# A conv, attention and expert kernel: the per-image matrix in twelve steps, another order of the set-up, and moved places in the slot

## The chip, the cores and the metric

The kernel runs on one core of a Trainium2 chip, from one launch. The metric is the time on the device in microseconds (us), lower is better. Each stated time of a kernel is the median of several runs.

## What is computed

The input x is 8 images of 56 x 56 pixels with 256 channels in float32, so 25,088 tokens of 256 numbers. Two layers follow each other. In the reference, cut to what matters:

```python
def _path(x, w1, ..., v3):                      # 32 of them, 4 inner channels each
    h = relu(_bn(einsum('nhwc,cd->nhwd', x, w1) + b1, ...))
    h = relu(_bn(conv3x3(h, w2) + b2, ...))
    return relu(_bn(einsum('nhwd,dc->nhwc', h, w3) + b3, ...))
x = relu(paths.sum(axis=0) + x)                 # layer 0

k, v = _layernorm(qkv, ...), _layernorm(qkv, ...)   # per head of 32 channels, q = qkv
kv = einsum('bhnd,bhne->bhde', k, v) / N            # one 32 x 32 matrix per head and image
out = einsum('bhnd,bhde->bhne', q, kv) + x          # attention without a softmax

probs = softmax(tokens @ router_w.T)                # 8 experts, the best 2 per token
for e in range(E):
    out = out + combine[:, e:e+1] * (gelu(tokens @ w1[e] + b1[e]) @ w2[e] + b2[e])

t = t + attention(_ln_t(t))                         # layer 1
t = t + experts(_ln_t(t))
```

## The kernel before, in words

**Tiles and slots.** The tokens are cut into 56 chunks of 448 (8 rows of an image, 7 chunks per image). The program is a loop over slots s (L1494 on). Slot s holds, interleaved: the third convolution (conv3) of chunk s as 32 `pair` steps (L631, products L643, relu on ACT L648, second relu and sum on DVE L651) with their sums on PE (`sum_paths`, L664, result u at L671); the first convolution (conv1, L265) of chunk s+2: transposes tx of the loaded xi (L276) and product c1 (L287); the taps R (L301) and the 3 x 3 convolution (conv2, L323) of chunk s+1, whose result is split in two parts and sent by DMA into hl (`halves`, L334); the end of chunk s-1 (`end_steps`, L693): transposes tu (L712), statistics per head, a power on POOL (L777), the inverse (up to L799), the scale on POOL (L803), and the products kv (L813), summed per image into kvs; and the attention of chunk a = s-8 (`attn_steps`, L920). Slots 0 to 7 have no attention; their places are those with "alone" in the name. Slots from 56 on have no convolution any more; they are the tail.

**Experts.** After attention, chunks are routed in groups of up to two (`route_steps`, L1018): DVE computes ranks up to rboth (L1067), PE multiplies it (rk, L1074), and rows go out to the experts' regions by indirect DMA from POOL (L1120). When a group of chunks is closed a plan (`plan_steps`, L1135, its run lists L1235 to L1256) makes the table of tiles of 128 rows. `moe_steps` then passes tiles through the experts' weights (te L1335, ph L1375, py L1391 and L1395), and the rows go back by indirect DMA (L1413).

**An image's matrix.** At slots 8, 15, 22, ..., 57 chunk a is the first of its image, and `image_steps` (L831) turns kvs into one 256 x 256 matrix in two halves f of 128 channels. `keys` (L835) makes, for each half, a diagonal matrix Arow of the channel sums (L847), its product with ones on PE (sv, L848), and with eight operations on DVE (L852 to L864) the half's A. Arow and At have one buffer each. `matrix` (L867) multiplies A by the mean and transposes it (cs, L872, and AT), and fills the table tab. `router` (L887) multiplies AT by the router's weights (ar), copies, multiplies by the mean (arm), subtracts. tab is what attention reads at L939.

**What sets the order.** PE, ACT and DVE run in the order in which the program issues (`manual_schedule`); POOL, SP and the DMA queues are ordered by the scheduler. Each list of steps gets places, fractions of the slot, from the dictionary `places` (L598 on): `at` gives each step its own place, other lists are spread by cost between two places, and `issue` sorts all steps of the slot by place and calls them. `after` in `places` says how many tile passes are left for each slot of the tail (`tiles_by`). PSUM has a pool of 7 buffers for all products but the sums.

**Set-up.** Before slot 0 the weights are loaded and laid out (W2s at L233 in twelve DMAs on the queue of SP), chunks 0 and 1 pass conv1, the mask and scale of the third weights are made (tp_mask, tp_g at L383, W3s at L384, tp_w at L391), then the table of the third bias (b4 at L414, tp_b3 at L419), and then conv2 of chunk 0. After that come the other tables, among them the centred router weights (tp_rw, L480). `load` (L84) fetches a chunk of x into xi.

Of the kernel before, what the change touches and what calls it, by code (L numbers as in the profile page):

```python
# [8 lines left out]
F32 = mybir.dt.float32  # L9
# [16 lines left out]
def kernel(  # L26
# [32 lines left out]
    P = 128  # L59
# [20 lines left out]


    xs_in = {}

    def load(s):  # L84
        b, c = divmod(s, NCH)
        X = xin.tile([T, KT, C], F32, tag="xi", name=f"xi_{s}")
        nc.sync.dma_start(
            out=X, in_=x[b, c * CH : (c + 1) * CH, :].rearrange("(k q) c -> q k c", q=T)
        )
        xs_in[s] = X  # L90

    xtp = ctx.enter_context(tc.tile_pool(name="xtp", bufs=4))
# [137 lines left out]
    W2s = setup.tile([3 * 32, NG, 3, D], F32, name="W2s")  # L230
    for dx in range(3):
        for g in range(NG):
            nc.sync.dma_start(  # L233
                out=W2s[dx : 3 * 32 : 3, g],
                in_=W2[32 * g : 32 * g + 32].rearrange(
                    "q (dy dx o) -> dx q dy o", dy=3, dx=3
                )[dx],
            )
# [76 lines left out]
    def conv2_steps(s):  # L315
# [19 lines left out]
        def halves():  # L335

            h2 = h2s[s]
            hi = split.tile([P, CH], F32R, tag="hi", name=f"hi_{s}")
            lo = split.tile([P, CH], F32R, tag="lo", name=f"lo_{s}")
            nc.vector.tensor_copy(hi, h2)  # L340
            nc.vector.tensor_tensor(lo, h2, hi.bitcast(F32), ALU.subtract)
# [46 lines left out]
    for ab in range(NQ):  # L388
# [9 lines left out]
            ALU.mult,  # L398
        )


    pmod = setup.tile([NP, NPL], F32, name="pmod")
    nc.vector.tensor_reduce(
# [12 lines left out]
        )  # L416
    tp = ps_mm.tile([P, 512], F32, tag="mm", name="tp_b3")
    for cg in range(NCG):
        nc.tensor.matmul(  # L419
            tp[:, cg * 8 : cg * 8 + 8],  # L420
            b4[:, cg].rearrange("q p c -> q (p c)"), pdiv, start=True, stop=True,
        )
    nc.vector.tensor_copy(b3t, tp[:, : NCG * 8].rearrange("q (g n) -> q g n", n=8))
    nc.vector.tensor_scalar_mul(nb3, b3t, -1.0)
    all_of(conv2_steps(0))

    for f in range(NF):
        tp = ps_mm.tile([P, 512], F32, tag="mm", name=f"tp_sb_{f}")
# [26 lines left out]
    tables = ctx.enter_context(tc.tile_pool(name="tables", bufs=1))  # L455


    def column(src, name):

        t = const.tile([P, NF], F32, name=name)  # L460
        nc.sync.dma_start(out=t, in_=src.rearrange("o (f c) -> c (o f)", c=P))
        return t

    def bcast(src, name):
        t = const.tile([P, C], F32, name=name)
        nc.sync.dma_start(out=t, in_=src.to_broadcast([P, C]))
        return t

    kw_c, kb_c = column(kw, "kw_c"), column(kb, "kb_c")
# [4 lines left out]
    nc.gpsimd.memset(mean_of, 1.0 / C)  # L474

    rwc = const.tile([P, NF, E], F32, name="rwc")
    nc.sync.dma_start(out=rwc, in_=rwT.rearrange("(f c) e -> c f e", c=P))
    tp = ps_mm.tile([P, 512], F32, tag="mm", name="tp_rw")
    for f in range(NF):
        nc.tensor.matmul(tp[:, :E], mean_of, rwc[:, f, :], start=(f == 0), stop=(f == NF - 1))  # L480
    for f in range(NF):
        nc.vector.tensor_sub(rwc[:, f, :], rwc[:, f, :], tp[:, :E])

# [106 lines left out]
    def unordered(ins, group, keep=()):  # L590
# [7 lines left out]


    places = {  # L600
        "after": [7, 5, 5, 5, 6, 5, 5, 5, 10],
        "attention": [0.108, 0.243, 0.378, 0.514, 0.622, 0.689, 0.744, 0.798, 0.881, 0.881],
        "attention first": [0.396, 0.487, 0.578, 0.669, 0.742, 0.953, 0.953, 0.953, 0.953, 0.989],
        "attention last": [
            0.151, 0.272, 0.393, 0.514, 0.611, 0.611, 0.657,
            0.706, 0.754, 0.791, 0.815, 0.839, 0.863, 0.912,
        ],
        "attention first last": [
            0.611, 0.692, 0.774, 0.856, 0.921, 0.962, 0.982,
            0.982, 0.982, 0.982, 0.982, 0.982, 0.982, 0.982,  # L610
        ],
        "conv1": [0, 0, 0.111],
        "conv1 alone": [0, 0.011, 0.024],
        "conv2": [0.615, 0.615, 0.655, 0.675],
        "conv2 alone": [0.607, 0.613, 0.613, 0.761],
        "end": [0.109, 0.151, 0.211, 0.242, 0.337, 0.431, 0.551, 0.681, 0.761, 0.908],
        "end alone": [0.143, 0.178, 0.188, 0.248, 0.328, 0.408, 0.408, 0.658, 0.752, 0.887],
        "fetch": [0.119],
        "image": [0.001, 0.107, 0.214],
        "tiles": [0.043, 0.2, 0.99],  # L620
        "conv3": [0.7, 0.9],
        "plan": [0.569, 0.983],
        "route": [0, 0.368],
        "route last": [0, 0.254],
        "scatter": [0.302, 0.551],
        "scatter last": [0.35],
        "taps": [0.144],
        "taps alone": [0.391],
    }

    unit, sums = {}, {}  # L631
# [199 lines left out]
    def image_steps(b):  # L831

        v = {}

        def keys():  # L835
            kv = kvs.pop(b)

            G3 = v["A"] = one.tile([P, NF, P], F32, tag="A", name=f"A_{b}")
            rows = one.tile([P, P], F32, tag="Arow", name=f"Arow_{b}")
            ps = ps_mm.tile([P, NF, P], F32, tag="mm", name=f"sv_{b}")  # L840
            for f in range(NF):

                g = kv[:, f, f : f + P]
                s = kv[:, f, P : P + 1] if f == 0 else kv[:, f, 0:1]
                vw, vb = vw_b[:, f * P : (f + 1) * P], vb_b[:, f * P : (f + 1) * P]

                nc.vector.tensor_scalar_mul(rows, ident, s)  # L847
                nc.tensor.matmul(ps[:, f, :], ones_f, rows, start=True, stop=True)  # L848

                A = G3[:, f, :]  # L850
                t = one.tile([P, P], F32, tag="At", name=f"At_{b}_{f}")
                nc.vector.tensor_mul(A, g, vw)  # L852
                nc.vector.scalar_tensor_tensor(A, vb, s, A, op0=ALU.mult, op1=ALU.add)
                nc.vector.tensor_scalar_mul(A, A, kw_c[:, f : f + 1])
                nc.vector.tensor_mul(t, vw, ps[:, f, :])
                nc.vector.scalar_tensor_tensor(t, vb, float(N), t, op0=ALU.mult, op1=ALU.add)
                nc.vector.scalar_tensor_tensor(
                    A, t, kb_c[:, f : f + 1], A, op0=ALU.mult, op1=ALU.add
                )
                nc.vector.scalar_tensor_tensor(  # L860
                    A, A, 1.0 / N, head_mask.rearrange("q h c -> q (h c)"),
                    op0=ALU.mult, op1=ALU.mult,
                )
                nc.vector.tensor_add(A, A, ident)  # L864

        def matrix():
            A = v["A"]  # L867
            ps = ps_mm.tile([P, NF, P], F32, tag="mm", name=f"cs_{b}")
            pt = ps_mm.tile([P, NF, P], F32, tag="mm", name=f"AT_{b}")
            AT = v["AT"] = one.tile([P, NF, P], F32, tag="AT", name=f"ATs_{b}")  # L870
            for f in range(NF):
                nc.tensor.matmul(ps[:, f, :], mean_of, A[:, f, :], start=True, stop=True)  # L872
                nc.tensor.transpose(pt[:, f, :], A[:, f, :], ident)
            tab = v["tab"] = one.tile(
                [P, NF, C + 2 * E], F32, tag="tab", name=f"tab_{b}", bufs=2
            )
            nc.vector.tensor_copy(AT, pt)
            for f in range(NF):
                for g in range(NF):
                    dst = tab[:, f, g * P : (g + 1) * P]  # L880
# [4 lines left out]
                nc.vector.tensor_copy(tab[:, f, C + E :], rwc[:, f, :])  # L885

        def router():  # L887
            AT, tab = v["AT"], v["tab"]
            ps = ps_mm.tile([P, 512], F32, tag="mm", name=f"ar_{b}")
            AR = one.tile([P, NF, E], F32, tag="AR", name=f"AR_{b}")  # L890
            for f in range(NF):
                nc.tensor.matmul(
                    ps[:, f * E : (f + 1) * E], AT[:, f, :], rwc[:, f, :], start=True, stop=True
                )
            nc.vector.tensor_copy(AR, ps[:, : NF * E].rearrange("q (f e) -> q f e", e=E))
            pm = ps_mm.tile([P, 512], F32, tag="mm", name=f"arm_{b}")
            for f in range(NF):
                nc.tensor.matmul(
                    pm[:, :E], mean_of, AR[:, f, :], start=(f == 0), stop=(f == NF - 1)
                )  # L900
            for f in range(NF):
                nc.vector.tensor_sub(tab[:, f, C : C + E], AR[:, f, :], pm[:, :E])
            tables_of[b] = tab

        return [(1.0, keys), (1.5, matrix), (1.0, router)]


    fetched, Xs, pays, logits = {}, {}, {}, {}
# [587 lines left out]
    for s in range(S + A + 1):  # L1496
# [116 lines left out]
```

## Time and profile before

| what | value |
|---|---|
| median of 3 runs | 3165.85 us (3164.92 to 3170.51) |
| the profiled run | 3194.13 us |
| its span in the trace | 3192.3 us, 1.83 us less than the run |
| granted PE clock, mean over the span | 0.962 |
| busy: PE, DVE, ACT, POOL | 92%, 68%, 60%, 58% of the span |
| set-up, 0 to 53 us | PE busy 27.39 us, PE clock 0.70 |
| tail, 2560 to 3192 us | PE busy 538.94 of 632 us |

In the profile PE is the matrix engine and PEld its loading of weights, DVE the vector engine, ACT the scalar engine, POOL the GpSimd engine and SP the engine that issues most DMAs. A row such as "L651 DVE ... x1792 | 1131.2, 677 | 446.4 <-ACT r L648 414.4" gives the line of the code, the engine, the operation, the count, the busy us and the mean ns of one; then the idle us of the engine just before such operations and what ended most of it. A row of the timeline gives start, length, and in brackets the idle time before it and what ended that. The profiled run is 0.9% above the median, so durations are read within its own span.

### The profile page before, as it was taken

What the parts mean: (1) busy time and instruction counts of PE and PEld (TensorE: products, weight loads), DVE (VectorE), ACT (ScalarE), POOL (GpSimd) and SP (SyncE); (2) the same over time, 40 slices, a digit from 0 to 9 for tenths busy, and PEclk for the clock granted to TensorE, in tenths of its full rate; (3) what the DMA queues carried; (4) which work ended last, traced back from release to release, by engine and by line L of the source; (5) the groups of instructions that cost most, each with busy time, mean ns of one, the idle gap of its engine ahead of it and who ended that gap; (6) DMA issues with size and microseconds to landing.
All of it is one profiled execution on the core that took longest, in us unless ns stands there. A gap on an engine that the chain in (4) does not pass through costs nothing.

```text
span 3192.3 us, 53679 instructions
## 1 busy us (share of the span) xinstructions
PE 2924.8 (92%) x16677; PEld 1663.9 (52%) x16677; DVE 2173.6 (68%) x5743; ACT 1919.8 (60%) x3827; POOL 1844.5 (58%) x1363
## 2 busy tenths in 40 slices
PE   6999888888999999999999999999999997887798
PEld 3334334333455555455555555555555555776677
DVE  4787887787877687776877777777778784433200
ACT  2666665556666666566666766566656654454455
POOL 1233254455566675756756666666663556677677
PEclk7999998899999999999999999999999998998899
DMA  2543344344556666667665766667756666898897
GB/s 68 156 127 123 120 133 127 112 146 152 158 163 163 190 175 177 168 177 192 184 184 155 203 184 169 179 164 197 191 161 181 176 160 152 210 250 205 202 223 179
DMA packets 322669, 537.53 MB, mean 168 GB/s; under 512 B 41152, under 2 KB 232784, under 8 KB 322384
## 3 DMA queue, kind: packets, MB, share of 16 engines
q1 hardware_dynamic: 239808, 429.91, 44.4%
q0 software_dynamic: 81984, 103.45, 17.8%
q8 instruction: 133, 2.18, 0.3%
q14 instruction: 152, 1.25, 0.1%
q10 hardware_dynamic: 592, 0.76, 0.1%
HBM read 248.01 MB, written 192.55 MB: 138 GB/s over the span
## 4 chain that ended last, share of the span: by engine, by line
PE 68%; DVE 10%; issue 4%; ACT 3%; POOL 3%; DMA 2%; another core or an unknown queue 0%; ACTq 0%; SPq 0%; POOLq 0%; DVEq 0%
PE c L643 12%; PE ph L1375 11%; PE su L664 11%; PE py L1395 9%; PE at L939 7%; PE kv L813 3%; DVE r L651 3%; PE te L1335 3%; PE c L323 2%; PE py L1391 2%; POOL hsd L777 2%; PE c L287 2%; ACT r L648 2%; PE tu L712 1%; PE tx L276 1%
## 5 line engine op out<-in xcount | busy, mean ns | idle before, releaser
L651 DVE SCALAR_TENSOR_TENSOR r<-c,nb,r 128x448 f32<-128x448 f32 x1792 | 1131.2, 677 | 446.4 <-ACT r L648 414.4
L648 ACT ACTIVATE r<-c,b3t 128x448 f32<-128x448 f32 x1792 | 1038.5, 634 | 333.0 <-PE c L643 314.9
L1413 POOL DMA_INDIRECT out_dram<-y,index x420 | 660.5, 1573 | 342.7 <-ACT y L1399 221.5
L643 PE MATMUL c<-hl,W3hl 64*128 64x448 f32 x3584 | 690.4, 427 | 52.7 <-ACT r L648 19.3
L1120 POOL DMA_INDIRECT regions<-pay,rrowi x448 | 428.9, 957 | 311.9 <-PE c L643 198.5
L664 PE MATMUL su<-r,gather 128*32 128x448 f32 x3584 | 558.0, 566 | 42.8 <-DVE r L651 34.6
L643 PEld LDWEIGHTS c<-hl,W3hl 64*128 64x128 f32 x3584 | 328.2, 188 | 482.6 <-issue 242.0
L1375 PE MATMUL ph<-eT,w 128*128 128x256 f32 x1680 | 453.2, 401 | 38.1 <-issue 15.1
L1399 ACT ACTIVATE y<-py,rows 128x256 f32<-128x256 f32 x420 | 196.7, 474 | 438.9 <-PE py L1395 327.8
L1395 PE MATMUL py<-w,hT 128*128 128x256 f32 x1680 | 432.0, 381 | 7.0 <-issue 6.3
L1375 PEld LDWEIGHTS ph<-eT,w 128*128 128x128 f32 x1680 | 306.0, 196 | 169.0 <-issue 77.0
L1379 ACT ACTIVATE hT<-ph,w 128x256 f32<-128x256 f32 x420 | 197.9, 476 | 252.2 <-PE ph L1375 127.6
L777 POOL TENSOR_TENSOR hsd<-hsd,half 112x36 f32<-112x36 f32 x49 | 303.3, 6190 | 70.5 <-DVE hsd L775 69.6
L1395 PEld LDWEIGHTS py<-w,hT 128*128 128x128 f32 x1680 | 290.3, 191 | 36.6 <-issue 7.5
L939 PE MATMUL at<-tab,tT 128*112 128x272 f32 x896 | 266.2, 421 | 15.1 <-ACT r L648 6.1
L738 POOL TENSOR_TENSOR norm<-t,hmean 112x512 f32<-112x512 f32 x112 | 121.4, 1164 | 245.5 <-PE c L643 125.0
L664 PEld LDWEIGHTS su<-r,gather 128*32 128x32 f32 x3584 | 101.6, 109 | 250.2 <-DVE r L651 107.9
L939 PEld LDWEIGHTS at<-tab,tT 128*112 128x112 f32 x896 | 150.8, 182 | 94.1 <-issue 33.1
L943 DVE SCALAR_TENSOR_TENSOR X<-at,rs,X 112x256 f32<-112x256 f32 x224 | 107.0, 478 | 122.4 <-PE at L939 60.8
L1391 PE MATMUL py<-b2hl,own 128*128 128x256 f32 x420 | 179.1, 426 | 6.7 <-ACT y L1399 2.8
L1065 POOL TENSOR_TENSOR rq<-ebase,rq 112x8 f32<-112x8 f32 (+1 forms) x32 | 51.2, 1600 | 227.0 <-DVE rq L1064 227.0
L1339 ACT COPY eT<-te 128x512 f32<-128x512 f32 x210 | 123.5, 588 | 60.5 <-PE te L1335 40.6
(261 smaller groups left out, 3160.4 us busy)
## 6 DMA issues: line engine op xcount, KB each, us to landing
w<-Wd SPq DMA_DIRECT2D x210, 513.0 KB
rows<-regions SPq DMA_DIRECT2D x210, 259.0 KB
xi<-in_x_dram SPq DMA_DIRECT2D x56, 448.0 KB
hl<-hi SPq DMA_DIRECT2D x112, 224.0 KB
tTs<-u SPq DMA_DIRECT2D x56, 448.0 KB
ts<-t SPq DMA_DIRECT2D x56, 448.0 KB
tT<-tTs SPq DMA_DIRECT2D x56, 448.0 KB
X<-ts SPq DMA_DIRECT2D x56, 448.0 KB
```

Of the source, the lines that this page charges most:

```text
L643: product = nc.tensor.matmul(tiles[g][:, :CH], W3hl[rows, ab, cg, :], hl[rows, ab, :], start=True, stop=True)
L648: nc.scalar.activation(r, tiles[0][:, :CH], AF.Relu, bias=b3t[:, cg, 2 * ab : 2 * ab + 1])
L651: nc.vector.scalar_tensor_tensor(r, tiles[1][:, :CH], nb3[:, cg, 2 * ab + 1 : 2 * ab + 2], r, op0=ALU.max, op1=ALU.add,)
L664: nc.tensor.matmul(ps[32 * c4 : 32 * c4 + 32, :CH], gather, unit.pop((s, 4 * u + c4)), start=(ab == 0), stop=(ab == NQ - 1),)
L777: nc.gpsimd.tensor_tensor(sd, sd, half[:T, :].rearrange("q (k h) -> q k h", k=KT), ALU.pow)
L939: nc.tensor.matmul(ps, tT[:, f, k * T : (k + 1) * T], tables_of[b][:, f, :], start=(f == 0), stop=(f == NF - 1),)
L1120: ins = nc.gpsimd.indirect_dma_start(out=regions[n], out_offset=bass.IndirectOffsetOnAxis(ap=v["row_i"][:, (m - group[0]) * KT + k, n : n ...
L1375: nc.tensor.matmul(ps, w[:, f * C + hf * P : f * C + (hf + 1) * P], eT[:, f, :], start=(f == 0), stop=(f == NF - 1),)
L1379: nc.scalar.activation(hT[:, hf, :], ps, AF.Gelu, bias=w[:, 2 * NF * C + hf : 2 * NF * C + hf + 1])
L1391: nc.tensor.matmul(ps, own.to_broadcast([P, P]), b2hl, start=True, stop=False)
L1395: nc.tensor.matmul(ps, hT[:, f, h * P : (h + 1) * P], w[:, (NF + f) * C : (NF + f + 1) * C], start=False, stop=(f == NF - 1),)
L1413: ins = nc.gpsimd.indirect_dma_start(out=out_rows, out_offset=at, in_=y[:, h, :], in_offset=None, compute_op=ALU.add, **partial,).ins
```

## The change

It has three parts.

1. `image_steps` returns twelve steps in place of three, each with a place of its own from 0.001 to 0.294 of the slot (before: 0.001, 0.107, 0.214). The diagonal matrices of both halves are made in the first step, in two buffers (the tags Arow and At), and both products sv follow in the second. No operation is added or left out.
2. Set-up: the twelve W2s DMAs are issued from POOL instead of SP. `conv2_steps(0)` is called before the table of the third bias. The load of chunk 3 waits for the split of chunk 0's conv2 (`halved`). The loads of kw, kb, vw, vb and of the router's weights wait for the last product of the bias table (`not_yet`). The centring of the router's weights moves to the start of slot 1.
3. Places: conv1 and conv2 with and without attention, the ends, attention, taps, plan, route, scatter and tiles, and the tile passes left for the tail (`after`, the sum goes from 53 to 52).

```diff
+        ins = nc.sync.dma_start(
             out=X, in_=x[b, c * CH : (c + 1) * CH, :].rearrange("(k q) c -> q k c", q=T)
-        )
+        ).ins
+        if s == 3:
+            tc.add_manual_dep(ins, halved[0].name, SYNC, reason="not needed by the first chunk")
...
-            nc.sync.dma_start(
+            nc.gpsimd.dma_start(
...
+            if s == 0:
+                halved.append(ins)
...
+    all_of(conv2_steps(0))
...
+    last_made = product.ins
     nc.vector.tensor_copy(b3t, tp[:, : NCG * 8].rearrange("q (g n) -> q g n", n=8))
     nc.vector.tensor_scalar_mul(nb3, b3t, -1.0)
-    all_of(conv2_steps(0))
...
+    def not_yet(ins):
+        tc.add_manual_dep(ins, last_made.name, SYNC, reason="not needed by the first chunk")
...
+    def center_router():
+        tp = ps_mm.tile([P, 512], F32, tag="mm", name="tp_rw")
+        for f in range(NF):
+            nc.tensor.matmul(tp[:, :E], mean_of, rwc[:, f, :], start=(f == 0), stop=(f == NF - 1))
+        for f in range(NF):
+            nc.vector.tensor_sub(rwc[:, f, :], rwc[:, f, :], tp[:, :E])
...
-        "after": [7, 5, 5, 5, 6, 5, 5, 5, 10],
-        "attention": [0.108, 0.243, 0.378, 0.514, 0.622, 0.689, 0.744, 0.798, 0.881, 0.881],
-        "attention first": [0.396, 0.487, 0.578, 0.669, 0.742, 0.953, 0.953, 0.953, 0.953, 0.989],
+        "after": [7, 5, 5, 3, 6, 5, 6, 5, 10],
+        "attention": [0.108, 0.235, 0.378, 0.514, 0.579, 0.689, 0.744, 0.798, 0.881, 0.94],
+        "attention first": [0.396, 0.487, 0.578, 0.669, 0.742, 0.953, 0.99, 0.99, 0.99, 0.99],
         "attention last": [
-            0.151, 0.272, 0.393, 0.514, 0.611, 0.611, 0.657,
-            0.706, 0.754, 0.791, 0.815, 0.839, 0.863, 0.912,
+            0.19, 0.311, 0.432, 0.553, 0.65, 0.65, 0.65,
+            0.693, 0.741, 0.778, 0.802, 0.938, 0.938, 0.938,
         ],
         "attention first last": [
             0.611, 0.692, 0.774, 0.856, 0.921, 0.962, 0.982,
             0.982, 0.982, 0.982, 0.982, 0.982, 0.982, 0.982,
         ],
         "conv1": [0, 0, 0.111],
-        "conv1 alone": [0, 0.011, 0.024],
-        "conv2": [0.615, 0.615, 0.655, 0.675],
-        "conv2 alone": [0.607, 0.613, 0.613, 0.761],
-        "end": [0.109, 0.151, 0.211, 0.242, 0.337, 0.431, 0.551, 0.681, 0.761, 0.908],
-        "end alone": [0.143, 0.178, 0.188, 0.248, 0.328, 0.408, 0.408, 0.658, 0.752, 0.887],
-        "fetch": [0.119],
-        "image": [0.001, 0.107, 0.214],
-        "tiles": [0.043, 0.2, 0.99],
+        "conv1 alone": [0, 0.003, 0.016],
+        "conv2": [0.621, 0.658, 0.658, 0.675],
+        "conv2 alone": [0.531, 0.629, 0.629, 0.806],
+        "end": [0.109, 0.151, 0.244, 0.244, 0.337, 0.431, 0.551, 0.681, 0.761, 0.908],
+        "end alone": [0.121, 0.156, 0.166, 0.226, 0.306, 0.386, 0.386, 0.636, 0.73, 0.865],
+        "fetch": [0.103],
+        "image": [
+            0.001, 0.028, 0.054, 0.081, 0.115, 0.134,
+            0.161, 0.187, 0.214, 0.241, 0.267, 0.294,
+        ],
+        "tiles": [0.029, 0.205, 0.99],
         "conv3": [0.7, 0.9],
-        "plan": [0.569, 0.983],
-        "route": [0, 0.368],
-        "route last": [0, 0.254],
-        "scatter": [0.302, 0.551],
+        "plan": [0.64, 0.983],
+        "route": [0.005, 0.373],
+        "route last": [0, 0.002],
+        "scatter": [0.302, 0.46],
         "scatter last": [0.35],
-        "taps": [0.144],
-        "taps alone": [0.391],
+        "taps": [0.124],
+        "taps alone": [0.413],
...
+        def ones_of(f):
+            kv = v["kv"]
+            return kv[:, f, P : P + 1] if f == 0 else kv[:, f, 0:1]
+        def rows():
+            v["kv"] = kvs.pop(b)
+            v["rows"] = [
+                one.tile([P, P], F32, tag=tag, name=f"{tag}_{b}") for tag in ("Arow", "At")
+            ]
             for f in range(NF):
+                nc.vector.tensor_scalar_mul(v["rows"][f], ident, ones_of(f))
+        def along():
+            ps = v["ps"] = ps_mm.tile([P, NF, P], F32, tag="mm", name=f"sv_{b}")
+            for f in range(NF):
+                nc.tensor.matmul(ps[:, f, :], ones_f, v["rows"][f], start=True, stop=True)
+            v["A"] = one.tile([P, NF, P], F32, tag="A", name=f"A_{b}")
+        def keys(f):
+            A = v["A"][:, f, :]
+            vw, vb = vw_b[:, f * P : (f + 1) * P], vb_b[:, f * P : (f + 1) * P]
+            nc.vector.tensor_mul(A, v["kv"][:, f, f : f + P], vw)
+            nc.vector.scalar_tensor_tensor(A, vb, ones_of(f), A, op0=ALU.mult, op1=ALU.add)
+            nc.vector.tensor_scalar_mul(A, A, kw_c[:, f : f + 1])
+        def values(f):
+            A = v["A"][:, f, :]
+            vw, vb = vw_b[:, f * P : (f + 1) * P], vb_b[:, f * P : (f + 1) * P]
+            t = one.tile([P, P], F32, tag="At", name=f"At_{b}_{f}")
+            nc.vector.tensor_mul(t, vw, v["ps"][:, f, :])
+            nc.vector.scalar_tensor_tensor(t, vb, float(N), t, op0=ALU.mult, op1=ALU.add)
+            nc.vector.scalar_tensor_tensor(
+                A, t, kb_c[:, f : f + 1], A, op0=ALU.mult, op1=ALU.add
+            )
+            nc.vector.scalar_tensor_tensor(
+                A, A, 1.0 / N, head_mask.rearrange("q h c -> q (h c)"),
+                op0=ALU.mult, op1=ALU.mult,
+            )
+            nc.vector.tensor_add(A, A, ident)
...
+        def turn():
             A = v["A"]
-            ps = ps_mm.tile([P, NF, P], F32, tag="mm", name=f"cs_{b}")
-            pt = ps_mm.tile([P, NF, P], F32, tag="mm", name=f"AT_{b}")
-            AT = v["AT"] = one.tile([P, NF, P], F32, tag="AT", name=f"ATs_{b}")
...
-        return [(1.0, keys), (1.5, matrix), (1.0, router)]
+        return [
+            (1.0, fn) for fn in (
+                rows, along, lambda: keys(0), lambda: keys(1), lambda: values(0),
+                lambda: values(1), turn, matrix, router, routed, mean, centered,
+            )
+        ]
...
+        if s == 1:
+            center_router()
```

More of the change, by code (lines that the diff above doesn't have):

```diff
@@ L82 @@
     xs_in = {}
+    halved = []
     def load(s):
@@ L232 @@
         for g in range(NG):
-            nc.sync.dma_start(
+            nc.gpsimd.dma_start(
                 out=W2s[dx : 3 * 32 : 3, g],
@@ L340, in halves @@
             nc.vector.tensor_copy(hi, h2)
-            nc.vector.tensor_tensor(lo, h2, hi.bitcast(F32), ALU.subtract)
+            ins = nc.vector.tensor_tensor(lo, h2, hi.bitcast(F32), ALU.subtract).ins
+            if s == 0:
+                halved.append(ins)
             hl = hlp.tile([P, NQ, CH], F32R, tag="hl", name=f"hl_{s}")
@@ L418 @@
     for cg in range(NCG):
-        nc.tensor.matmul(
+        product = nc.tensor.matmul(
             tp[:, cg * 8 : cg * 8 + 8],
@@ L455 @@
     tables = ctx.enter_context(tc.tile_pool(name="tables", bufs=1))
+    def not_yet(ins):
+        tc.add_manual_dep(ins, last_made.name, SYNC, reason="not needed by the first chunk")
     def column(src, name):
         t = const.tile([P, NF], F32, name=name)
-        nc.sync.dma_start(out=t, in_=src.rearrange("o (f c) -> c (o f)", c=P))
+        not_yet(
+            nc.sync.dma_start(out=t, in_=src.rearrange("o (f c) -> c (o f)", c=P)).ins
+        )
         return t
@@ L465, in bcast @@
         t = const.tile([P, C], F32, name=name)
-        nc.sync.dma_start(out=t, in_=src.to_broadcast([P, C]))
+        not_yet(nc.sync.dma_start(out=t, in_=src.to_broadcast([P, C])).ins)
         return t
@@ L476 @@
     rwc = const.tile([P, NF, E], F32, name="rwc")
[L477 to L482, printed above, removed]
+    not_yet(nc.sync.dma_start(out=rwc, in_=rwT.rearrange("(f c) e -> c f e", c=P)).ins)
+    def center_router():
[4 more added lines that the diff above has]
+            nc.vector.tensor_sub(rwc[:, f, :], rwc[:, f, :], tp[:, :E])
     TR = 2 * P
@@ L833, in image_steps @@
         v = {}
[L835 to L840, printed above, removed]
-            for f in range(NF):
[L843 to L864, printed above, removed]
@@ L866, in matrix @@
-        def matrix():
+        def ones_of(f):
[6 more added lines that the diff above has]
+            ]
+            for f in range(NF):
+                nc.vector.tensor_scalar_mul(v["rows"][f], ident, ones_of(f))
[4 more added lines that the diff above has]
+            v["A"] = one.tile([P, NF, P], F32, tag="A", name=f"A_{b}")
@@ L867, in matrix @@
+        def turn():
             A = v["A"]
-            ps = ps_mm.tile([P, NF, P], F32, tag="mm", name=f"cs_{b}")
-            pt = ps_mm.tile([P, NF, P], F32, tag="mm", name=f"AT_{b}")
-            AT = v["AT"] = one.tile([P, NF, P], F32, tag="AT", name=f"ATs_{b}")
+            ps = v["cs"] = ps_mm.tile([P, NF, P], F32, tag="mm", name=f"cs_{b}")
+            pt = v["pt"] = ps_mm.tile([P, NF, P], F32, tag="mm", name=f"AT_{b}")
             for f in range(NF):
@@ L873, in matrix @@
                 nc.tensor.transpose(pt[:, f, :], A[:, f, :], ident)
+        def matrix():
+            A, ps = v["A"], v["cs"]
+            AT = v["AT"] = one.tile([P, NF, P], F32, tag="AT", name=f"ATs_{b}")
             tab = v["tab"] = one.tile(
@@ L876, in matrix @@
             )
-            nc.vector.tensor_copy(AT, pt)
+            nc.vector.tensor_copy(AT, v["pt"])
             for f in range(NF):
@@ L887, in router, with routed, mean, centered @@
         def router():
-            AT, tab = v["AT"], v["tab"]
-            ps = ps_mm.tile([P, 512], F32, tag="mm", name=f"ar_{b}")
-            AR = one.tile([P, NF, E], F32, tag="AR", name=f"AR_{b}")
+            ps = v["ar"] = ps_mm.tile([P, 512], F32, tag="mm", name=f"ar_{b}")
             for f in range(NF):
                 nc.tensor.matmul(
-                    ps[:, f * E : (f + 1) * E], AT[:, f, :], rwc[:, f, :], start=True, stop=True
-                )
-            nc.vector.tensor_copy(AR, ps[:, : NF * E].rearrange("q (f e) -> q f e", e=E))
-            pm = ps_mm.tile([P, 512], F32, tag="mm", name=f"arm_{b}")
+                    ps[:, f * E : (f + 1) * E], v["AT"][:, f, :], rwc[:, f, :],
+                    start=True, stop=True,
+                )
+        def routed():
+            AR = v["AR"] = one.tile([P, NF, E], F32, tag="AR", name=f"AR_{b}")
+            nc.vector.tensor_copy(AR, v["ar"][:, : NF * E].rearrange("q (f e) -> q f e", e=E))
+        def mean():
+            pm = v["pm"] = ps_mm.tile([P, 512], F32, tag="mm", name=f"arm_{b}")
             for f in range(NF):
                 nc.tensor.matmul(
-                    pm[:, :E], mean_of, AR[:, f, :], start=(f == 0), stop=(f == NF - 1)
+                    pm[:, :E], mean_of, v["AR"][:, f, :], start=(f == 0), stop=(f == NF - 1)
                 )
+        def centered():
+            tab = v["tab"]
             for f in range(NF):
-                nc.vector.tensor_sub(tab[:, f, C : C + E], AR[:, f, :], pm[:, :E])
+                nc.vector.tensor_sub(tab[:, f, C : C + E], v["AR"][:, f, :], v["pm"][:, :E])
             tables_of[b] = tab
-        return [(1.0, keys), (1.5, matrix), (1.0, router)]
+        return [
+            (1.0, fn) for fn in (
+                rows, along, lambda: keys(0), lambda: keys(1), lambda: values(0),
+                lambda: values(1), turn, matrix, router, routed, mean, centered,
+            )
+        ]
     fetched, Xs, pays, logits = {}, {}, {}, {}
```

## The prediction

> **What bounds the kernel now.** I read the page first (engine shares, then the chain that ended last), then the busy time in windows cut at the stages, then PE's list of waits, and last the timelines of the set-up, of the fourth image's opening and of one plan.
>
> ```profile
> PE 2924.8 (92%) x16677; PEld 1663.9 (52%) x16677; DVE 2173.6 (68%) x5743; ACT 1919.8 (60%) x3827; POOL 1844.5 (58%) x1363
> ...
> L1120 POOL DMA_INDIRECT regions<-pay,rrowi x448 | 428.9, 957 | 311.9 <-PE c L643 198.5
> ```
>
> PE has 92% of the span, and the chain gives it 68%. The second row is POOL's own indirect transfer, kept as a price. By stage (window, us, then busy us of PE, PEld, DVE, ACT, POOL, then granted PE clock, DMA share, GB/s):
>
> ```profile
> 53.00:322.00 269.00, 249.00 (x1472) 104.85 (x1472) 209.76 (x385) 180.79 (x322) 74.51 (x38) 0.99 0.42 125
> 1207.03:1256.53 49.50, 49.36 (x287) 27.42 (x287) 34.83 (x72) 33.22 (x68) 31.87 (x21) 1.00 0.70 188
> 1301.00:1652.00 351.00, 339.97 (x2008) 187.11 (x2008) 263.17 (x676) 228.78 (x460) 227.72 (x156) 0.99 0.67 180
> 2800.00:2900.00 100.00, 77.40 (x381) 63.49 (x380) 33.33 (x169) 45.43 (x104) 75.86 (x60) 0.89 0.85 224
> ```
>
> The second row is one plain slot (27): PE idles 0.14 of 49.50 us. There a new place can only avoid new stalls. What can be won lies in the set-up (0 to 53 us: PE busy 27.4), where an image opens, where a plan falls, and in the tail (2560 to 3192 us: PE busy 539 of 632). An image opens so (start, us, instruction, idle before it and its releaser):
>
> ```profile
> 1301.73 0.46 PE L848 MATMUL sv<-Arow,ones_f 128*128 128x128 f32 x2 [1.21 <-DVE Arow L847]
> 1304.31 0.49 PE L848 MATMUL sv<-Arow,ones_f 128*128 128x128 f32 x2 [2.12 <-DVE Arow L847]
> ```
>
> The second row-sum product waits until DVE has built all of the first half of A, since both halves use one Arow buffer and one step. In the whole trace this wait costs 25.2 us in 15 waits. The clock pays too, in the first window below, and after a single stall of 1.30 us elsewhere in the second:
>
> ```profile
> 1304.50:1306.00 1.50, 1.50 (x7) 0.83 (x7) 1.40 (x5) 0.51 (x1) 0.00 (x0) 0.59 1.03 206
> 1325.00:1330.00 5.00, 5.00 (x21) 2.77 (x21) 4.27 (x14) 1.51 (x3) 4.08 (x4) 0.66 0.69 171
> ```
>
> **Set-up.**
>
> ```profile
> 35.90 3.55 PE L419 MATMUL tp_b<-pdiv,b 32*128 32x8 f32 x16 [2.92 <-DVE b L414]
> 39.38 4.71 PE L323 MATMUL c<-R,W2t 96*32 96x448 f32 x24
> ...
> 52.91 1.12 PE L643 MATMUL c<-hl,W3hl 64*128 64x448 f32 x4 [5.93 <-DMA hl<-hi]
> ```
>
> Conv2 of chunk 0 (39.38) stands behind the b3 table, whose product waited for DVE. It now goes ahead: tp_w ends at 32.98, so conv2 gains up to 39.38 - 32.98 = 6.4 us. Its halves then go to hl, and the table is made while they travel.
>
> The twelve W2s loads leave SP, where issuing them took 7.71 us (from 7.66) and the second xi came after (PE waited 7.91 for it). On POOL I take the L1120 row: 0.957 us each plus the 0.30 us issue gap seen between two of them, so 12 x 1.25 = 15 us from about 5.3. With its memsets and masks after them POOL ends near 24.6; tp_mask and tp_g follow at about 26.0 instead of 26.7, so tp_w ends near 32.3 and conv2 gains 39.4 - 32.3 = 7.1. [...]
>
> After conv2, tx and c1 of chunk 2 now come before the first pairs, +0.5 us; tp_rw (1.02 us at the low clock) goes to slot 1, -0.7. The waits added to xi 3 and to kw, kb, vw, vb, rwc stand on SP: behind them are only loads first used at slot 1 or later, taken at nothing; if that cover fails, up to 2 us. Sum -7; bounds -12 (0.6 us per transfer, the hl chain then last) and +2 (2 us each).
>
> **Image openings, eight.** Before: 1.21 + 2.12 idle, and 3.6 us of work at about half clock, 1.8 lost: with 0.3 of small gaps, 5.4 us. After: no operation is gone. Arow and At are made together, so both sv run at about 1301.8 after one wait of 1.2. The second stall goes; next late is cs, which needs all of A. DVE, from its rows: both diagonals to 1301.75; the waiting parts of the pair (r) to 1303.4; logit and index 0.5; keys 0.91 twice, u 0.68 between; best 1.0; the next r 1.3; values 1.57 twice: A complete near 1311.8, against 1308.9 before, because route steps and pairs now lie between. PE in that time has te 0.66, su 0.96, ph 1.03, pairs 0.67 twice, c1 1.67 and tu 0.65 from 1302.3, so it is done near 1308.6 and waits about 3.2 us at cs. [...] The rows show 0.59 after these gaps and 0.66 after 1.30, so each stall pays; I take 1.8 again. After: 1.2 x 0.4 + 3.2 + 1.8 = 5.5 less some work pulled ahead of the stall: by the time of rk (1319.3) I find about -0.5 each, x 8 = -4. Bounds: every stall gone, -5.1 x 8 = -41; A's end even later than I count, +1.7 x 8 = +14.
>
> **Slots 1 to 7 (no attention).** In the 53 to 322 window PE idles 20 of 269. c1 follows tx at once and may wait 0.5 us for xT; the split of conv2 covers the 0.83 us wait of su; tu comes in one piece, +0.9 less. Taken at 0, bounds +-1 x 7. **Plain slots**: conv2, tu, tiles move within a PE-full slot, nothing to gain, 0; the 6.19 us pow on POOL (L777) has the same fill before it in either order. **Plans**: moved from 0.569 to 0.64, what they collide with changes:
>
> ```profile
> 1191.26 2.79 DVE L1244 SCALAR_TENSOR_TENSOR run<-iot,run 128x14 f32<-128x14 f32 x1
> ...
> 1191.82 2.19 POOL L988 TENSOR_TENSOR X<-X,pay 112x1024 f32<-112x1024 f32 x1
> ```
>
> DVE's 0.17 us operation lasts 2.79 beside POOL's, the pairs behind it wait on DVE, and kv on PE idles 2.94. Seen twice (4.35 and 2.9 us idle of PE), and five waits for count, 6.5 us. Some go, others may come: -3, bounds +-8. **Tail**: the last two routes start at the slot's beginning and end sooner; PE waits 9.14 us there for rk. But rk now stands early in PE's order while DVE needs some 4 to 5 us for rboth. One tile pass (4.1 us of PE) moves to the full part. The tail idles 93 us, of which the edit touches perhaps 30: -6, bounds +-15.
>
> **Sum**: -7 - 4 + 0 - 3 - 6 = -20. The profiled run took 3194.13 (span 3192.3, 1.83 around), 28.3 above the median of 3165.85; on it I expect 3174, on the median 3165.85 - 20 = 3146.
>
> **Rivals.** (1) The image stalls vanish: A is done before PE reaches cs. For: DVE is idle a fifth of these slots, and a tile pass can fill PE. Against: my count of DVE above. -41 - 7 - 8 = 3110. (2) Nothing is gained: the POOL transfers cost near 2 us, and the stall at sv only moves to cs. For: no operation is removed; DVE has the same sum. 3166 +- 6. (3) Slower: in the new order the plan's run operations follow the inverse (L799) directly, and that releases POOL's scale of norm (L803, two of 1.20 us). The first 13 of the 17 plans (the rest lie in the tail) then hold DVE some 2.8 us as L1244 did, PE idles, and the clock costs 1.5: 13 x 4.3 = +56, less 20: about 3200. It decides once L803 starts within 0.3 us of L799, which POOL does when its queue is empty. Against: before, only 2 of these 13 met POOL so, and PE has pairs buffered.
>
> **How the numbers follow.** A measurement of this kernel can tell about 0.2%, 6.3 us, from no change: under 3159.5 is faster, over 3172.2 slower. Likeliest case 0.50 (own range 3130 to 3162: 0.45 faster, 0.05 same); rival 1 0.30, faster; rival 2 0.11 (0.05 faster, 0.05 same, 0.01 slower); rival 3 0.09 (0.08 slower, 0.01 same). Sums: 0.80, 0.11, 0.09. The range 3105 to 3168 takes in the likeliest case, most of rival 1 and of rival 2, and leaves rival 3 out: about 0.17 outside.
>
> **What would show it.** Set-up: conv2 of chunk 0 starts near 32, the first pair near 46; W2s on POOL at about 1.25 us each. Image: sv with one wait of 1.2 us, then cs waiting about 3 us for A (none in rival 1), clock below 0.7 after it. Plans: L1244 at 0.2 us as a rule (2.8 in rival 3). Tail: rk waits under 9 us. I am wrong if the twelve transfers take over 2 us each, if cs doesn't wait, or if plain slots lengthen from 49.5.

## The result: 3166.73 to 3130.26 us

Timed beside the kernel before, the changed kernel has a median of 3130.26 us (3127.16 to 3142.2, 4 runs) against 3166.73 us: a ratio of 0.9887, 95% interval 0.9867 to 0.9908, 36 us less. 3146 was forecast. The profiled run of after is the fastest of its four; its page says:

```profile
PE 2882.5 (92%) x16677; PEld 1642.7 (53%) x16677; DVE 2167.8 (69%) x5743; ACT 1915.7 (61%) x3827; POOL 1850.4 (59%) x1375
...
L1165 POOL DMA_INDIRECT regions<-pay,rrowi x448 | 429.3, 958 | 302.2 <-PE c L660 173.4 <-issue 70.1 <-PE py L1440 14.6
```

PE executes the same 16,677 matmuls and is busy 42 us less than in the first trace of before. No work is gone; the same matmuls ran at a higher clock (0.973 over the span, 0.962 before). In both traces the granted clock is 1.00 or 0.50 and nothing between, so PE spent about 169 us at half clock instead of 243 (an estimate: twice the span times one less clock), which is worth 37 of the 42 us. The indirect transfer costs what it did.

In the set-up (PE's timeline of after):

```profile
16.97 0.69 PE L388 MATMUL tp_g<-g,spread 32*128 32x256 f32 x2 [0.90 <-ACT spread L386]
...
25.44 2.46 PE L326 MATMUL c<-R,W2t 96*32 96x448 f32 x24
31.08 3.45 PE L425 MATMUL tp_b<-pdiv,b 32*128 32x8 f32 x16 [3.18 <-DVE b L420]
...
38.89 3.21 PE L660 MATMUL c<-hl,W3hl 64*128 64x448 f32 x12
```

tp_g is at 16.97 (25.98 in the first trace of before), conv2 at 25.44 (39.38) and ahead of the bias table, the first pair at 38.89 (52.91). Conv2 also runs in 2.46 us instead of 4.71, at a granted clock of 1.00 instead of 0.50. The loads moved to POOL cost far less than the row that I had taken (group of after: busy us, mean ns):

```profile
L236 POOL DMA_DIRECT2D W2s<-in_W_dram x12 | 6.9, 577 | 0.0
```

The fourth image opens so:

```profile
1266.86 0.46 PE L869 MATMUL sv<-Arow,ones_f 128*128 128x128 f32 x2 [0.41 <-DVE Arow L864]
1267.16 0.39 PE L869 MATMUL sv<-At,ones_f 128*128 128x128 f32 x2
...
1275.06 0.49 PE L901 MATMUL cs<-A,mean_of 128*128 128x128 f32 x2 [0.56 <-DVE A L894]
...
1276.62 0.49 PE L901 MATMUL cs<-A,mean_of 128*128 128x128 f32 x2 [0.97 <-DVE A L894]
```

The wait has moved from sv to cs and has become smaller: 0.41 + 0.56 + 0.97 us in place of 1.21 + 2.12.

To see where time goes, I follow the start of DVE's operation u (before L671, after L688), two per chunk, through each trace: the first u of chunk s less the first u of chunk s-1 is "slot s" below, and the span less the last u is "the tail".

### The profile page after: what moved, and what is told of

It reads as the page before. It is cut to its first block, busy times and chain, and to the rows that moved or that the text cites. A ratio compares the mean times of both kernels' runs of the same rounds, so it can differ in the third digit from the quotient of the medians.

```text
span 3125.4 us, 53728 instructions
## 1 busy us (share of the span) xinstructions
PE 2882.5 (92%) x16677; PEld 1642.7 (53%) x16677; DVE 2167.8 (69%) x5743; ACT 1915.7 (61%) x3827; POOL 1850.4 (59%) x1375
## 3 DMA queue, kind: packets, MB, share of 16 engines
q14 instruction: 154, 1.25, 0.1%
## 5 line engine op out<-in xcount | busy, mean ns | idle before, releaser
L681 PE MATMUL su<-r,gather 128*32 128x448 f32 x3584 | 532.6, 566 | 37.8 <-DVE r L668 33.9
L1420 PEld LDWEIGHTS ph<-eT,w 128*128 128x128 f32 x1680 | 298.7, 193 | 164.4 <-issue 45.9
L984 PE MATMUL at<-tab,tT 128*112 128x272 f32 x896 | 258.1, 411 | 14.5 <-ACT r L665 8.3
L1436 PEld LDWEIGHTS py<-b2hl,own 128*128 128x128 f32 x420 | 79.7, 190 | 146.2 <-ACT r L665 45.6
L326 PE MATMUL c<-R,W2t 96*32 96x448 f32 x1344 | 149.3, 546 | 0.1
```

What stands on the lines that cost most here:

```text
L681: nc.tensor.matmul(ps[32 * c4 : 32 * c4 + 32, :CH], gather, unit.pop((s, 4 * u + c4)), start=(ab == 0), stop=(ab == NQ - 1),)
L984: nc.tensor.matmul(ps, tT[:, f, k * T : (k + 1) * T], tables_of[b][:, f, :], start=(f == 0), stop=(f == NF - 1),)
L1420: nc.tensor.matmul(ps, w[:, f * C + hf * P : f * C + (hf + 1) * P], eT[:, f, :], start=(f == 0), stop=(f == NF - 1),)
L1436: nc.tensor.matmul(ps, own.to_broadcast([P, P]), b2hl, start=True, stop=False)
```

## Experiments

All kernels ran beside the kernel before; each row's change is the ratio less one, times 3167. PE busy and idle are from each profile, as differences from e1 (span 3161.6, PE busy 2912.4, idle 249.2); each is of one execution, and the two of the kernel before differ by 12 us in PE busy.

| run | what | median us | ratio (95%) | change us | PE busy, idle |
|---|---|---|---|---|---|
| e1 | before, again | 3167.07 | 1.0000 (0.9989 to 1.0011) | 0 | 0, 0 |
| e2 | before + set-up | 3148.39 | 0.9948 (0.9934 to 0.9962) | -16 | -2, -12 |
| e3 | before + image steps | 3179.59 | 1.0040 (1.0027 to 1.0054) | +13 | +21, -4 |
| e4 | before + places | 3151.38 | 0.9956 (0.9943 to 0.9969) | -14 | -18, +6 |
| e10 | e4, places of conv, ends, attention, tiles only | 3141.83 | 0.9912 (0.9899 to 0.9925) | -28 | -7, -14 |
| e11 | e4, the other places only | 3193.05 | 1.0071 (1.0055 to 1.0086) | +22 | +7, +28 |
| after | all | 3130.26 | 0.9887 (0.9867 to 0.9908) | -36 | -30, -6 |
| e5 | after, three image steps | 3133.46 | 0.9893 (0.9871 to 0.9915) | -34 | -31, 0 |
| e6 | after, W2s on SP | 3139.94 | 0.9905 (0.9888 to 0.9921) | -30 | -26, -5 |
| e7 | after, conv2 behind the bias table | 3134.13 | 0.9887 (0.9868 to 0.9905) | -36 | -23, -5 |
| e8 | after, image's last steps later | 3120.12 | 0.9844 (0.9827 to 0.9861) | -49 | -24, -20 |
| e9 | after, old tail | 3125.04 | 0.9861 (0.9847 to 0.9875) | -44 | -18, -20 |
| e12 | e8, last routes over 0.12 of the slot | 3124.59 | 0.9854 (0.9840 to 0.9869) | -46 | -12, -25 |

**e1, the kernel before once more**, no edit.

> The kernel before, unchanged, for a second profile. Theory A (the first profiled run, 3194 us, was 28 us over its median, and part of the 67 us between the two traces is that run alone): the span is now 3160 to 3172, and slots differ from the first trace where stalls are a matter of chance (plans, tail); set-up and image openings are the same to 0.5 us. Theory B (the trace was typical and the spans differ by 67): span above 3185. Ratio 1.000 in both.

```profile
span 3161.6 us, 53679 instructions
```

Theory A, but for the set-up: chunk 0's u comes at 68.8 us instead of 71.2, so that part too differs by more than 0.5. The span is 30.7 us under the first trace's. Slot 27 takes 50.38 us in place of 55.11, the image slots 29 and 36 take 55.58 and 55.37 in place of 57.09 and 57.07, and the longest run operation of a plan (L1244) is 1.81 us, with a wait of 1.95 us on PE behind it. Of the two stalls behind plans that I had read as a cost of the plan's place (4.35 and 2.94 us), e1 has only this shorter one. From here on e1 is the trace to compare with.

**e2, the set-up alone**: the diff's edits outside of places and image steps.

> Only the set-up edits on the kernel before. Theory A (the 17.2 us by which chunk 0 is done sooner are kept to the end): 0.9945, -17 us; first conv3 product near 39 instead of 52.9. Theory B (given back, as the slots after 9 wait for POOL and the tail for DMA): within 5 us of before.

Theory A: -16 us, so the gain is kept. Chunk 0's u comes at 54.1 instead of 68.8. In the trace this lead of 14.7 us falls to 10.8 by slot 15, most of it at slot 14 (3.6 us), and the tail is 4.2 us shorter.

**e6 and e7, the set-up's two halves**, each undone on after.

```diff
-            nc.gpsimd.dma_start(
+            nc.sync.dma_start(
...
-    all_of(conv2_steps(0))
 
     pmod = setup.tile([NP, NPL], F32, name="pmod")
...
     nc.vector.tensor_scalar_mul(nb3, b3t, -1.0)
+    all_of(conv2_steps(0))
```

> The kernel after, with the twelve W2s loads back on SP; all else new. Theory A (they held up the second xi, and POOL issues them at 0.54 us each without harm): the second tx at 19 instead of 12, the first conv3 product near 46 instead of 38.9, +7 us, 0.991 of before. Theory B (conv2's place alone made the gain): first conv3 product within 1 us of 38.9, same time as after.

> The kernel after, with conv2 of chunk 0 back behind the bias table. Theory A (PE's queue: the table's 3.2 us wait and 3.5 us of products stand ahead of conv2): first conv3 product 5 to 7 us later than 38.9, +6 us, 0.9905 of before. Theory B (the halves' DMA and the table overlap in either order): within 2 us of after.

PE's timeline of e6, then of e7:

```profile
18.93 1.76 PE L279 MATMUL tx<-ident,xi 112*128 112x112 f32 x8 [7.75 <-DMA xi<-in_x_dram]
```

```profile
28.48 3.55 PE L423 MATMUL tp_b<-pdiv,b 32*128 32x8 f32 x16 [2.92 <-DVE b L418]
31.96 4.71 PE L326 MATMUL c<-R,W2t 96*32 96x448 f32 x24
```

In the traces both are theory A: with W2s on SP the second chunk's xi comes 7 us later (tx at 18.93, not 12.09), and chunk 0's u is 7.9 us later than in after; with the table ahead, conv2 starts at 31.96, and that u is 5.6 us later, of which 2.25 are conv2's own length (4.71 us, which it also takes in before at a clock of 0.50, and 2.46 in after at 1.00). In the times, e6 loses 6 us against after and e7 none, with intervals that overlap: neither half is shown there by itself, only the 16 us of the whole set-up in e2.

**e3, the twelve image steps alone.**

```diff
+        "image": [0.001, 0.028, 0.054, 0.081, 0.115, 0.134, 0.161, 0.187, 0.214, 0.241, 0.267, 0.294],
...
+        return [(1.0, fn) for fn in (rows, along, ..., mean, centered)]
```

> Only the twelve image steps with their places on the kernel before. Theory A (the traces: image slots shorter by 2.3 us each on the mean): -18 us, 0.994; waits at sv under 4 us in all, at cs 15. Theory B (the recorded forecast: -0.5 each): -4 us, 0.999.

Neither theory: 13 us slower. The waits at sv fall by 22.2 us, as planned, but PE's list of waits now has

```profile
PE cs L887 <- DVE A L880: 17.1, 16, 2.2
...
PE arm L921 <- DVE AR L916: 7.2, 6, 2.0
```

arm is new at this size (2.5 in e1): AR's copy has its own place among DVE's other work. 17.1 + 7.2, with 2.9 left at sv, take the place of 25.1 + 2.5, so hardly any idle time is gone on the whole (-4), and PE is busy 21 us longer. From the first u of slot 7 to that of slot 19, in e1 and then in e3 (length, busy PE, PEld, DVE, ACT, POOL, clock, DMA share, GB/s):

```profile
305.44:827.79 522.35, 456.24 (x2640) 209.41 (x2640) 416.07 (x1045) 314.01 (x597) 243.21 (x167) 0.93 0.44 132
304.85:841.04 536.19, 469.65 (x2640) 218.16 (x2640) 417.54 (x1045) 313.76 (x596) 243.08 (x167) 0.89 0.43 129
```

The stretch is 13.8 us longer for the same 2,640 matmuls; PE idles 66.1 and 66.5 us in it, and the clock is 0.93 and 0.89. In slot 8 of e3, behind a 2.00 us wait at arm (334.82):

```profile
334.00:338.00 4.00, 3.18 (x16) 1.38 (x16) 3.04 (x6) 1.16 (x2) 1.82 (x2) 0.64 0.18 62
338.00:342.00 4.00, 4.00 (x15) 2.35 (x12) 2.72 (x7) 3.04 (x6) 0.23 (x1) 0.50 0.00 0
```

The clock column is where the loss is, and it is not this one trace's: the mean clock is 0.960 to 0.963 in seven of e3's eight timed runs and 0.971 in the eighth, its fastest with 3169.55 us; e1's twelve have 0.963 to 0.970.

**e5, all but the image steps**: after with `(1.0, keys), (1.5, matrix), (1.0, router)` and `"image": [0.001, 0.107, 0.214]`.

> The kernel after, with the image steps put back to three at the old places; set-up and all other places are the new ones. Theory A (the split pays only with the new places around it: -36.5 less -20 for the set-up and -17 for the places leaves about 0 to -6 for it): 0 to 6 us slower than after, 0.9885 to 0.991 of before. Theory B (it costs 11 us here too, as alone): 0.985. Theory C (it carries much of the gain): slower than after by over 10, above 0.992.

Theory A: within the new places the split is worth 0.0006, 2 us, less than the intervals can tell. Seven image slots (8 to 50) together take 376.1 us in e1, 376.1 in e5, and 375.2 in after.

**e8, the wait at cs taken away**: a block of su and a ph stand ahead of cs, in PE's order.

```diff
         "image": [
             0.001, 0.028, 0.054, 0.081, 0.115, 0.134,
-            0.161, 0.187, 0.214, 0.241, 0.267, 0.294,
+            0.2, 0.22, 0.245, 0.262, 0.285, 0.305,
         ],
```

> The kernel after, with the image's last six steps later: 0.2, 0.22, 0.245, 0.262, 0.285, 0.305 for 0.161 to 0.294, so that a block of su and ph stands ahead of cs. Theory A (PE loses some 1.9 us at cs and several us at half clock after it, eight times): the waits at cs go from 15.3 to under 4 us and 10 to 25 us are gained over after, 0.981 to 0.9855 of before. Theory B (DVE is the limit here, the stall moves to su or arm): within 4 us of after.

Theory A. PE's list of waits, in after and in e8:

```profile
PE cs L901 <- DVE A L894: 15.3, 16, 1.8
```

```profile
PE cs L901 <- DVE A L894: 3.1, 5, 0.9
```

The seven image slots fall from 375.2 to 359.9 us, and the ratio from 0.9887 to 0.9844, with intervals that don't meet: 14 us. e12, with the same image steps, has 361.0 us. This is the fastest kernel of the study by its median. So the split pays once what waits for its last product is late enough. Three image steps with their later ones moved back likewise were not run; in that form the wait is at sv (25.2 us in e5), ahead of the steps that e8 moves.

**e4, e10 and e11, the places.** e10 and e11 split e4: e10 has conv1, conv2, taps, end, attention, fetch and tiles; e11 has plan, route, scatter, the tail's entries and the list `after`.

> Only the places on the kernel before, the image steps at their old three places. Theory A (what is left of -36 after set-up -17 and image -18): within 5 us of before. Theory B (set-up or image given back, and the plans and the tail carry the gain): -10 to -20 us.

> The kernel before, with only the places of conv1, conv2, taps, ends, attention, fetch and tiles new. Theory A (the gain of the places, 14 to 17 us, is made where the slots are not yet full of PE work, by fewer and shorter stretches at low clock): 8 to 14 us faster than before, 0.9955 to 0.9975. Theory B (it is made in plans, routes and the tail): within 5 us of before.

> The kernel before, with only the places of plan, route and scatter, the tail's entries and the tile passes left new. Theory A: 2 to 7 us faster than before, 0.998 to 0.9993. Theory B: 12 to 17 us faster, 0.995 to 0.996.

e4 gives 14 us, theory B's number. But its reason falls with the halves: e10 alone gives 28 us, twice the whole, and e11 alone costs 22. For e10 theory A has the place right (slots that are not full of PE work) and half of the size; both theories of e11 are wrong. In e10 PE's wait of su for r goes from 39.2 us (35 times) to 23.3 (16 times), while that of c for r grows from 4.2 to 10.9; half of the gain is there by slot 19 (11 of 24 us at the last u), the rest comes at about 0.4 us a slot. In e11 waits for r and for rboth grow (su 52.0, rk 22.5 in place of 9.5), and its loss comes in steps, at slots 10 and 20 (3.7 and 3.6 us), 36, 37, 44, 50 and 51 (some 3 us each come back at 32, 39 and 48), and once more between the last two u (e9 shows that one). Slot 10 is worth a look, since PE stalls there as in e1. In e11:

```profile
395.08 1.19 PE L664 MATMUL su<-r,gather 128*32 128x448 f32 x3 [2.25 <-DVE r L651]
```

```profile
392.69:396.10 3.41, 1.16 (x6) 0.27 (x4) 2.23 (x6) 1.29 (x3) 2.63 (x3) 1.00 0.57 214
396.10:399.51 3.41, 3.41 (x12) 1.54 (x11) 1.82 (x4) 1.78 (x4) 0.60 (x2) 0.50 0.00 0
```

In e1:

```profile
394.04 1.53 PE L664 MATMUL su<-r,gather 128*32 128x448 f32 x4 [2.25 <-DVE r L651]
```

```profile
389.02:392.43 3.41, 2.45 (x13) 0.81 (x12) 1.49 (x3) 2.69 (x7) 3.41 (x1) 1.00 0.36 134
392.43:395.84 3.41, 1.80 (x8) 0.60 (x10) 2.92 (x7) 0.51 (x2) 2.39 (x3) 1.00 0.36 136
395.84:399.25 3.41, 2.94 (x24) 2.20 (x20) 2.32 (x4) 2.70 (x5) 1.52 (x1) 1.00 0.02 5
```

The same stall of 2.25 us costs clock in one trace and none in the other. The windows above are cut where the clock can change: within each of the 14 traces (before, after, e1 to e12) all changes of the granted clock lie on a grid of 3.413 us (to 0.003 us), and where the grid begins differs from trace to trace. In e11 the whole stall falls into one step of the grid, with PE busy 1.16 of 3.41 us; in e1 it falls across two, with 2.45 and 1.80. Counted over the 14 traces, a step at full clock with PE busy under 40% is followed by one at half clock in 266 of 266 cases, from 40% to 80% in 196 of 992, above 80% in 3 of 10,784. So a slot of one trace that is 2 to 4 us longer than in another is no evidence by itself, and only the timed runs settle what e11's list costs. Its steps at 36 to 51 are not traced to single stalls.

**e9, the tail's entries old again**, on after: attention last, route last, and `"after": [7, 5, 5, 5, 6, 5, 5, 5, 10]`.

> The kernel after, with the tail's entries old: attention last, route last, and 53 instead of 52 tile passes left. Theory A (they give one tile pass of 4 us and a few us of stalls): 3 to 8 us slower than after, 0.990 to 0.9915 of before. Theory B (rk at the head of PE's list, with its wait of 9.7 us, costs what the rest gives): same as after or faster, 0.9885 or less.

Theory B: without these entries after is not slower. By the ratios it is 8 us faster (0.9861 against 0.9887), but the intervals just overlap and the two traces differ by 1.8 us. In slot 56, the first with "route last", PE's timeline shows what the new place does, in after and then in e9:

```profile
2606.87 0.68 PE L660 MATMUL c<-hl,W3hl 64*128 64x448 f32 x4
2613.32 0.26 PE L1119 MATMUL rk<-rboth,earlier 112*112 112x128 bf16 x1 [5.78 <-DVE rboth L1112]
```

```profile
2605.65 0.95 PE L681 MATMUL su<-r,gather 128*32 128x448 f32 x4
2606.96 1.53 PE L681 MATMUL su<-r,gather 128*32 128x448 f32 x4 [0.36 <-DVE r L668]
2608.42 1.17 PE L984 MATMUL at<-tab,tT 128*112 128x272 f32 x4
...
2613.50 0.26 PE L1119 MATMUL rk<-rboth,earlier 112*112 112x128 bf16 x1 [2.59 <-DVE rboth L1112]
```

In after rk stands at the head of the slot: PE waits 5.78 us for rboth with the last sums and the attention products queued behind it, and the clock is 0.50 in the 4 us after. In e9 these go first, the last u starts at 2608.53 instead of 2616.53, and PE still waits 2.59 us at rk. rk itself runs at the same time in both: the new place brings no route forward, since DVE sets when rboth is ready. Little of these 8 us is left in the end: after the last u the tail takes 508.9 us in after and 515.1 in e9, where the rest of the wait for rboth, rk itself and one tile pass more come behind that u.

**e12, the last routes later**, on e8.

```diff
-        "route last": [0, 0.002],
+        "route last": [0, 0.12],
```

> The kernel with the image's last six steps later (the fastest so far), and the last routes spread over 0 to 0.12 of the slot instead of 0 to 0.002. Theory A (PE waits up to 11 us for rboth at the head of its list; behind te and ph the wait is covered): rk waits under 6 us in the tail, 3 to 8 us faster than without, 0.982 to 0.9835 of before. Theory B (what ends late in the tail is the rows that follow rk, so a later rk delays them): same or slower, 0.984 to 0.986.

PE's waits in the tail, e8 and then e12:

```profile
PE rk L1119 <- DVE rboth L1112: 20.3, 4, 11.0
```

```profile
PE rk L1119 <- DVE rboth L1112: 13.3, 5, 3.6
```

The long wait of 11.0 us goes, as theory A has it, and these waits fall by 7.0 us in all. But others come, and PE is busy 12 us longer; the last u comes 2.3 us earlier, and the tail after it grows from 506.6 to 515.4 us: theory B by the time. The median is 4 us slower, within the intervals: no gain, and whether there is a loss stays open.

## Why the prediction held, and where its steps failed

The direction and the range were right: -36 us where -20 was forecast. The sum is right for partly wrong reasons, and in part by luck: two of its terms, measured alone, missed by 28 and 31 us in opposite directions.

- **Set-up, forecast -7, measured -16 (e2).** The mechanism held; one term was mis-sized. I priced a load on POOL at 1.25 us, by the indirect transfer of 957 ns; it took 0.577 us (ten of them in 5.43), below my lower bound of 0.6. By the row's price POOL would have had its masks done near 24.6; path_mask was done at 15.7, and tp_g started at 16.97 instead of 25.98, conv2 at 25.44 where 32 was forecast. So the second xi's earlier arrival, of which the forecast let 0.7 us through, was the larger half (7.9 us in e6's trace, conv2's place 5.6 in e7's). The sum also left out the clock: up to chunk 0's u it is 0.78 in e1 and 0.87 in e2. The ten loads ran beside a DVE that was busy 4.07 of the 5.43 us, with operations of at most 0.37 us. No run shows the 0.6 or the 2 us for each transfer that the forecast's bounds use; after shows 0.577 on the mean, 0.545 to 0.807.
- **Image openings, forecast -4, measured about -2 in company (e5), +13 alone (e3).** "Next late is cs" held: A is complete 9.7 us after sv's start (forecast 10.0). The stall that I put at 3.2 us is 1.53: PE arrives 0.8 us later, held up by ACT's h, and the first half's cs and AT (0.6 us) run while the second half is made. The forecast's own sum was 5.5 us after against 5.4 before; the -0.5 for each opening came from work pulled ahead, for which it gave no working. That the split gains little is right; e8 shows what was left there. Rival 1 (-41) did not happen.
- **Plain slots, forecast 0, measured -28 with the rest of those places (e10).** This step failed. "PE is full, nothing to gain" was read from one slot and holds about there (slot 28: 48.64 us in e1, 47.95 in e10), but not for slots 8 to 19, where PE idles 66.1 of 522.4 us in e1 and e10 gains 8.7 us, nor for the many short waits of su for r. Set-up and these places alone, -16 and -28, would be more than the whole change gives.
- **Plans, routes and tail, forecast -9, measured +22 alone (e11) and +14 beside e10's places (e4 against e10); the tail's entries in after 0 to +8 (e9).** This step failed too, on the other side, and hides the step above. I had named the mechanism, "rk now stands early in PE's order while DVE needs some 4 to 5 us for rboth", and set no price on it: it is 5.78 us in slot 56 and half clock after, and the longest wait at rk is 9.7 us, where under 9 was forecast. "One tile pass moves to the full part" was counted as a gain; it is work moved, and costs PE about the same there as in the tail (in after te 0.66 and 0.60 us, four py 1.02 and 1.03). By the rows of before's timeline it is nearer 4.9 us than the 4.1 that I took (an estimate from starts: te 0.6, ph twice 0.95, py twice 1.2). And of the plans' stalls that I hoped to save, e1 has one of 1.95 us. No run has the plans' places alone.
- **Rival 3 (plans under POOL's scale)** did not happen: the operation that took 2.79 us before (L1244, now L1289) takes at most 0.244 us in after, and the longest of all run operations 0.755.
- **The clock.** That short stalls cost clock, which I took from the rows of before (0.59 behind the waits of 1.21 and 2.12 us at sv, 0.66 behind one of 1.30), stands: behind the 2.25 us stall of e11 the clock is 0.50. But 1.8 us per stall was too regular a price. A step at half clock is worth at most 1.7 us of PE's work (an estimate, half of 3.41), and whether a stall brings one depends on how it falls into the grid (slot 10: PE busy 1.16 of 3.41 us in e11's one step, 2.45 and 1.80 in e1's two): in the 20 us behind the first sv of each of the eight openings, the clock is 0.83 to 0.91 in e1 and 0.74 to 1.00 in after.

Open: why the image steps cost 13 us alone and nothing with the new places. That the loss is in the clock of slots 8 to 19 is shown, and the wait at arm (7.2 us in e3, 2.5 in after) is one difference; the 21 us of slower matmuls are not traced to single stalls. Nor do the parts add: -16, +13 and -14 make -17, and together they gave -36. A kernel with the set-up, e10's places, e8's image and the old routes and tail was not tried.

## What to carry to other kernels

Splitting a step moved its stall to the next consumer here, and paid when that consumer was placed behind enough other work; so look for the new first waiter and move it as well. Price a queue by transfers of the same kind (0.577 us here where 0.957 stood for it), and get a second profile before a single stall is put down to a place in the program. Test groups of tuned constants apart: a total of -14 was made of -28 and +22, which don't simply add. An instruction moved forward in PE's list gained nothing where DVE set when its input was ready (rk at 2613.32 us in after, 2613.50 in e9); it only made all behind it wait, 5.78 us. What one stall costs in clock is in part luck, as slot 10 shows (a clock of 1.00 behind it in e1, 0.50 in e11), so compare the mean clocks of many runs.

## What was not expected of the hardware

A direct load issued from POOL took 0.577 us, its indirect transfer 0.958. The same 2.25 us stall of PE left the granted clock at 1.00 in one trace and took it to 0.50 for 6.8 us in another: in all 14 traces it changed only on a grid of 3.413 us, and every step at full clock with PE busy under 40% was followed by one at half clock (266 of 266). Two profiles of one kernel differed by 30.7 us in span, 12.4 of them in PE's busy time for the same matmuls.
